# Window attention: queries of strips 2 to 5 written over y between routing and the first pair

## The chip, the cores and the metric

The kernel runs on one core of a Trainium2 chip. A core has five engines with an instruction queue each, worked off in order: PE (TensorE: matmuls and transposes; PEld is its weight loads), DVE (VectorE), ACT (ScalarE), POOL (GpSimd) and SP (SyncE, here used to issue DMAs and to load registers). SBUF is the on-chip memory of 128 partitions, PSUM the small memory that PE writes and DVE and ACT read. Engines wait for each other by semaphores.

The metric is the device time of one execution in microseconds (us), the median of the runs shown. The profile is one execution recorded by the hardware profiler. Its span is the time from the first to the last recorded instruction.

## The reference, cut to what matters

Input and output are 4 images of 64 x 64 pixels with 256 channels. Four residual layers follow one another: two attention layers of the same form, then a Mamba layer and a grouped Mamba layer, which the change does not touch. One attention layer is, with other names shortened:

```python
Z = tanh(w2a @ tanh(w1a @ gn(x)))          # 1x1 convolutions, biases left out
F = sigmoid(w2b @ tanh(w1b @ gn(x)))
y = scan(h = F * h + (1 - F) * Z)          # along H, half of the channels flipped
q, k, v = split(windows(y) @ qkv_w.T)      # 64 windows of 8 x 8 pixels
idx = top_k(mean(q) @ mean(k).T, 4)        # routing: 4 key windows for each window
o = softmax(q @ k[idx].T * SCALE) @ v[idx] # 8 heads of 32 channels, 64 x 256 scores
out = wo_w @ (o + depthwise_conv3x3(v))    # nine taps a channel ("lepe")
x = x + out
```

## The kernel before, in words

The batches run in sequence, and within each the two attention layers and the Mamba layers. All data are float32. 256 channels lie as two halves (`m` = 0, 1) of 128 partitions. The image is cut into 8 **strips** of 8 columns (512 pixels); a strip holds 8 windows. `y`, `x` and `vimg` (the values, with a margin for the 3x3 convolution) stay in SBUF.

The order of instructions on each engine is the order in which the Python code issues them: it is written out by hand, and there is no scheduler. The tile framework adds the semaphore waits; a tile with `bufs=n` has n buffers that are used in turn.

An attention layer has three parts.

**Scan phase** (`scan_phase`, strips s = 0 to 7). Each step makes four pairs of 1x1 convolutions on PE (`conv`, L204: one is 128x512 outputs over 256 inputs), with ACT's tanh as eviction (L283), scans the strip into `y` on DVE, and then makes keys and values of the strip before (`keys_values`), whose rows go to `kv_dram` by DMA (L332, L351). Convolutions use five PSUM buffers with the tag `mm`. From s = 3 on DVE also works on the depthwise convolution of strip s - 3 (`lepe`: 18 steps, 9 for each half; L238 the first tap, L240 the others, accumulated in PSUM). In steps 5 and 6 the queries of strips 0 and 1 are made: `queries` returns an `evict` (two ACT instructions of 64x512, L261) and a `double` (two DMAs of 128 KB, L270). Doubling is there because each of the two 64-partition halves of q has to meet keys that lie in either half of the partitions: `qbuf[s % 2][m]` holds q for both.

**Routing** (`routing`). From window sums of y, q and k means are made, their products, and DVE finds the four best windows (`idx`, L424). After it, DVE makes half m = 0 of strip 5's depthwise convolution (nine taps in PSUM).

**Window phase** (`window_phase`). 32 **pairs** of windows, i = 4 x strip + a. The work of pair i is:

- `indices` (L446): SP loads the eight window numbers into registers. `gather` (L459): eight DMAs of 128 KB fetch keys and values (tile `kv`, six buffers: three pairs). For pairs 0 and 1 ACT's queue issues half of them.
- `scores` (L483): 64 matmuls into two PSUM tiles `sc`, each with one head half h.
- `smallest` (L493): DVE, the minimum of each row of `sc` (q is stored negated), for h = 0 and 1.
- `exps` (L504): eight ACT exponentials with a sum. The last one of each h frees its `sc` tile.
- `normalise`: DVE's reciprocal (L516), then eight POOL products (L519).
- `turn` (L532): 16 PE transposes to PSUM; `turned`: copies to SBUF, two on DVE (L543), two on ACT (L545).
- `values` (L558): 64 matmuls; `own_rows` (L569): DVE adds the result to `vimg`.

In the loop, iteration i issues the gather of pair i + 2, the doubling DMAs, the register loads of i + 3, the scores, minima, exps and normalise of i + 1, and the turn and values of i. Into the same loop go: the queries of strips 2 to 7 (`queries` for m = 0 of strip sj + 2 at a = 3, for m = 1 of strip sj + 1 at a = 0; the evictions at the end of the iteration, the doubling DMAs in the next one, after its gather), the output projection of the strip before (`project`, L204, `add` L579), and the depthwise taps of strips 6 and 7 on POOL (two instructions a tap, L225 and L226). The nine taps of half m = 1 of strip 5 are DVE instructions that add in place in `vimg` (`early`): three between `scores(0)` and the first `smallest`, two at the end of each of the iterations 0, 1 and 2:

```python
mids, ends, left = {}, {0: early[3:5], 1: early[5:7], 2: early[7:]}, []
```

Of the kernel before, what the change touches and what calls it, by code (L numbers as in the profile page):

```python
# [8 lines left out]
F32 = mybir.dt.float32  # L9
BF16 = mybir.dt.bfloat16  # L10
U32 = mybir.dt.uint32
AF = mybir.ActivationFunctionType
# [32 lines left out]
class Net:  # L45
# [33 lines left out]
    def attention_layers(self, x, w_drams, v_drams):  # L79
        tc, nc = self.tc, self.nc  # L80
        with ExitStack() as ctx:
# [13 lines left out]
            nc.gpsimd.memset(vimg[:, :, S + 9 : S + 10, :], 0.0)  # L95


            qbuf = [
                [big.tile([P, 2, NW, 64], F32, name=f"q{i}{m}") for m in range(2)]
                for i in range(2)  # L100
            ]
            layers = []
            for i in range(2):
                vec = wp.tile([P, ATT_VEC], F32, name=f"att_v{i}")
# [93 lines left out]
                return gn(dict(xn={}), s, psum, eng, self.gvar[:, 4 * s : 4 * s + 4])  # L198


            def conv(psum, w, w0, src, m):
                ps = psum.tile([P, NT], F32, tag="mm", name="conv_ps")
                for k in range(2):
                    nc.tensor.matmul(  # L204
                        ps, w[:, k, w0 + m * P : w0 + (m + 1) * P], src[:, k],
                        start=(k == 0), stop=(k == 1),
                    )
                return ps
# [41 lines left out]
            kvd = dram.tile([NW * NW, 64, 2 * C], F32, name="kv_dram")  # L250
            kvd_w = kvd.rearrange("(a b) p f -> b p a f", b=NW)

            def queries(lay, s, m, psum):
                src = y[:, :, strip[s], :].rearrange("p c w h -> p c (w h)")
                ps = conv(psum, lay["wb"], WQ - 4 * C, src, m)
                q = qbuf[s % 2][m]

                def evict():
                    for b in range(2):
                        rows = slice(b * 64, b * 64 + 64)  # L260
                        nc.scalar.activation(  # L261
                            q[rows, b].rearrange("p w (j i) -> p w j i", i=8),
                            ps[rows].rearrange("p (j w i) -> p w j i", j=8, i=8),
                            AF.Identity, bias=lay["neg_bq"][rows, m : m + 1], scale=-SCALE,
                        )

                def double():
                    for b in range(2):
                        here, there = slice(b * 64, b * 64 + 64), slice(64 - b * 64, 128 - b * 64)
                        nc.sync.dma_start(q[there, b], q[here, b])  # L270

                return evict, double


            def scan_phase(lay, work, psum, tail):
# [78 lines left out]
                doubles = []  # L354
                for s in range(NW):
                    g = gn_four(lay, s + 2, lambda: psum) if s + 2 < NW else [lambda: None] * 4
                    taps = lepe(lay, s - 3, psum) if s >= 3 else []
                    g[0]()
                    xn = lay["xn"].pop(s).rearrange("p c w h -> p c (w h)")
                    ha, ha_half = hidden("ha", W1A, xn, AF.Tanh, vec[:, B1A : B1A + 2])  # L360
                    hb, hb_half = hidden("hb", W1B, xn, AF.Tanh, vec[:, B1B : B1B + 2])
                    z, z_half = hidden("z", W2A, ha, AF.Tanh, vec[:, B2A : B2A + 2])

                    f, f_half = hidden("f", W2B, hb, AF.Tanh, lay["half_b2b"], scale=0.5)
                    for half in (ha_half, hb_half):
                        half(0)
# [12 lines left out]
                    g[2]()  # L379
                    f_half(0)  # L380
                    f_half(1)
                    scan(s, f, z)
                    if s:
                        keys_values(s - 1)
                    g[3]()
                    if s >= 5:
                        for _, double in doubles:
                            double()
                    doubles = [queries(lay, s - 5, m, psum) for m in range(2)] if s in (5, 6) else []
                    for evict, _ in doubles:  # L390
                        evict()
                keys_values(NW - 1)


# [34 lines left out]
            def window_phase(lay, work, psum, idx, nxt):  # L429
# [40 lines left out]
                def scores(i):  # L470
                    sj, a = divmod(i, 4)
                    if i < n_pair:
                        for h in range(2):
                            sc[h] = psum.tile([P, 2, 2, 2, P], F32, tag="sc", name="sc", bufs=2)
                        for w in range(2):
                            for m in range(2):
                                for r in range(2):
                                    for h in range(2):
                                        r0 = r * 64 + h * 32
                                        rows = slice(r0, r0 + 32)  # L480
                                        for b in range(2):
                                            k0 = b * P + m * 64
                                            nc.tensor.matmul(  # L483
                                                sc[h][b * 64 : b * 64 + 64, r, w, m, :],
                                                qbuf[sj % 2][m][rows, b, 2 * a + w],
                                                kv[i, w][rows, :, k0 : k0 + 64],
                                                start=True, stop=True,
                                            )
# [111 lines left out]
                mids, ends, left = {}, {0: early[3:5], 1: early[5:7], 2: early[7:]}, []  # L600

                def plan(steps, *where):
                    for f, (at, i) in zip(steps, where):
# [11 lines left out]
                else:  # L615

                    for s in range(NW - 1):
                        i = 4 * s + (10 if s < 5 else 7)
                        plan(stats(s, lambda: psum), (ends, 4 * s + 6), (ends, i), (mids, i + 1),
                             (ends, i + 2), (mids, i + 3), (ends, i + 3), (mids, i + 4))  # L620
                double = None
                for i in range(n_pair):
                    sj, a = divmod(i, 4)
                    add = evict = None
                    gather(i + 2)
                    if double:
                        double()
                        double = None
                    indices(i + 3)
                    scores(i + 1)  # L630
                    smallest(i + 1, 0)
# [50 lines left out]
            for i, lay in enumerate(layers):  # L682
                with tc.tile_pool(name=f"at_a{i}", bufs=1, reuse_waits="tile") as work, tc.tile_pool(
# [1399 lines left out]
```

## Time and profile before

| what | value |
|---|---|
| median of 3 runs | 12012.73 us (11994.23 to 12017.54) |
| the profiled execution | 11996.08 us |
| its span | 11993.8 us |
| TensorE clock granted, mean | 0.93 |
| busy: PE | 9862.3 us (82%) |
| busy: DVE | 9842.8 us (82%) |
| busy: POOL | 8892.2 us (74%) |
| busy: ACT | 7047.9 us (59%) |
| from the first minimum (L493) of a layer to its last, mean of 8 layers | 247.7 us |

The eight attention layers take up about a third of the span; the rest are the Mamba layers, which dominate the page's list of costly groups. A group's line reads: source line, engine, operation, tiles written and read, shapes, count | busy time, mean ns of one | idle time of the engine just before, and what ended most of it. A timeline's line reads: start, duration, engine, line, operation, tiles, shapes, count [idle before <- what ended it]; neighbouring instructions of one kind are drawn together. A line of waits reads: engine and line <- what it waited for: us in total, times, longest. PE's records show two matmuls for each float32 matmul of the program.

### The profile page before, as it was taken

To read this page: it belongs to the slowest core of one execution; us is meant where nothing else is said; L and a number is where in the kernel's file an instruction comes from. 1 tells how busy PE (TensorE), PEld (TensorE's weight loads), DVE (VectorE), ACT (ScalarE), POOL (GpSimd) and SP (SyncE) were. 2 spreads that over 40 slices of the span, in tenths; PEclk is the share of its full clock that TensorE was granted. 3 is DMA by queue.
4 is the path that set the end of the run, shared out by engine and by line. 5 is a ranking of instruction groups with operands and counts; after the bars stand their busy time and mean duration, and the time that the engine had idled before them with its cause. 6 is when DMAs were issued, how large, how long until landed. Compare 5 with 4: busy or idle time off the path is not lost. (4 is left out here: it accounts for less than half of the span.)

```text
span 11993.8 us, 192457 instructions
## 1 busy us (share of the span) xinstructions
PE 9862.3 (82%) x70632; PEld 5605.7 (47%) x71104; DVE 9842.8 (82%) x8322; ACT 7047.9 (59%) x13064; POOL 8892.2 (74%) x6082
## 2 busy tenths in 40 slices
PE   8988887777898788777789878877778987887777
PEld 4554554444455455444445545544444554554444
DVE  6677998998666799899866679989986667998998
ACT  4555555776455555477645655547764565555776
POOL 3666886898466688689846668868974666886897
PEclk9998998999999999899999989989999998998999
DMA  3343444554334355445433444445543343554454
GB/s 92 104 124 134 175 173 146 173 180 161 87 104 126 135 173 175 147 168 179 160 87 104 128 135 173 176 145 169 182 160 84 101 127 134 173 174 147 169 174 155
DMA packets 682830, 1742.11 MB, mean 145 GB/s; under 512 B 89216, under 2 KB 195216, under 8 KB 681632
## 3 DMA queue, kind: packets, MB, share of 16 engines
q1 hardware_dynamic: 676768, 1721.39, 43.4%
q8 instruction: 563, 9.22, 0.3%
q10 hardware_dynamic: 5120, 8.39, 0.3%
q14 instruction: 379, 3.10, 0.1%
HBM read 1601.51 MB, written 94.37 MB: 141 GB/s over the span
## 5 line engine op out<-in xcount | busy, mean ns | idle before, releaser
L927 POOL TENSOR_TENSOR hc<-h,cb 128x1024 f32<-128x1024 f32 x2056 | 4812.2, 2352 | 805.6 <-DVE h L921 358.3
L921 DVE TENSOR_TENSOR_SCAN h<-da,m_state,pb 128x1024 f32<-128x1024 f32 x1248 | 2920.3, 2340 | 163.2 <-DVE pb L915 1.5
L873 PE MATMUL y<-ident,hc 128*128 128x128 f32 x16384 | 2353.3, 291 | 449.9 <-POOL hc L927 351.9
L873 PEld LDWEIGHTS y<-ident,hc 128*128 128x128 f32 x16384 | 2052.7, 151 | 1128.6 <-POOL hc L927 574.4
L915 DVE TENSOR_TENSOR pb<-du,pb 128x1024 f32<-128x1024 f32 x1672 | 2024.8, 1211 | 122.3 <-PE pb L845 98.9
L857 ACT ACTIVATE da<-delta,m_v 128x1024 f32<-128x1024 f32 x1672 | 1898.9, 1141 | 135.8 <-DVE h L921 119.7
L845 PE MATMUL pb<-m_parts,pick 128*128 128x512 bf16 x2840 | 973.1, 413 | 824.0 <-DVE h L921 766.5
L519 POOL TENSOR_SCALAR pr<-pr,sm,zero 128x256 f32<-128x256 f32 x2048 | 1131.3, 569 | 412.1 <-DVE sm L516 362.2
L504 ACT ACTIVATE pr<-sc,mn 128x256 f32<-128x256 f32 x2048 | 959.8, 493 | 717.2 <-DVE mn L493 351.1
L845 PEld LDWEIGHTS <-pick 128*128 128x128 bf16 x3312 | 262.9, 101 | 1770.5 <-DVE h L921 972.9
L921 DVE TENSOR_TENSOR_SCAN h<-da,pb 128x1024 f32<-128x1024 f32 x424 | 969.7, 2287 | 54.9 <-DVE pb L915 1.0
L831 POOL TENSOR_TENSOR bb<-du,bb 128x1024 f32<-128x1024 f32 x376 | 889.0, 2364 | 101.5 <-DMA bb<-m_cd 94.1
L493 DVE TENSOR_REDUCE mn<-sc 128x4 f32<-128x1024 f32 x512 | 609.4, 1219 | 352.7 <-PE sc L483 352.6
L921 DVE TENSOR_TENSOR_SCAN h<-dap,m_state,bb 128x1024 f32<-128x1024 f32 x288 | 672.2, 2334 | 69.2 <-ACT dap L857 48.4
L532 PE MATMUL pt_ps<-ident,pr 128*128 128x128 f32 x4096 | 590.6, 286 | 135.1 <-ACT pts L545 100.3
L204 PE MATMUL conv_ps<-att_y,att_wb 128*128 128x512 f32 x1536 | 691.4, 594 | 5.3 <-DVE gn_mean L151 5.3
L532 PEld LDWEIGHTS pt_ps<-ident,pr 128*128 128x128 f32 x4096 | 459.4, 144 | 361.7 <-POOL tap L225 102.8
L857 ACT ACTIVATE dap<-delta,m_v 128x1024 f32<-128x1024 f32 x376 | 419.7, 1116 | 314.1 <-DVE h L921 232.1
L483 PE MATMUL sc<-kv,q 32*64 32x128 f32 x16384 | 401.4, 296 | 155.7 <-DMA kv<-kv_dram 90.8
L558 PE MATMUL ov_ps<-pts,kv 128*32 128x64 f32 x16384 | 427.8, 231 | 122.1 <-DVE pts L543 74.1
L240 DVE SCALAR_TENSOR_TENSOR lp<-vimg,att_v,lp 128x512 f32<-128x512 f32 x616 | 465.5, 756 | 27.9 <-DVE lp L240 0.5
L204 PE MATMUL conv_ps<-att_xn,att_wa 128*128 128x512 f32 x1024 | 462.7, 605 | 14.2 <-POOL att_xn L180 14.2
(289 smaller groups left out, 16960.3 us busy)
## 6 DMA issues: line engine op xcount, KB each, us to landing
cb<-m_cd SPq DMA_DIRECT2D x2048, 512.0 KB, 3.8
kv<-kv_dram SPq DMA_DIRECT2D x1984, 128.0 KB, 2.7
bb<-m_cd SPq DMA_DIRECT2D x376, 512.0 KB, 5.1
kv_dram<-kst SPq DMA_DIRECT2D x128, 256.0 KB, 3.4
kv_dram<-vn SPq DMA_DIRECT2D x128, 256.0 KB, 4.2
q<-q SPq DMA_DIRECT2D x256, 128.0 KB, 3.0
m_pe<-in_pe_dram SPq DMA_DIRECT2D x32, 512.0 KB, 6.2
out_dram<-yo SPq DMA_DIRECT2D x64, 256.0 KB, 2.4
```

The lines of the kernel that those rows point to most:

```text
L204: nc.tensor.matmul(ps, w[:, k, w0 + m * P : w0 + (m + 1) * P], src[:, k], start=(k == 0), stop=(k == 1),)
L493: nc.vector.tensor_reduce(mn[h], sc[h].rearrange("p r w m n -> p (w m) r n"), AX.XY, ALU.min)
L504: nc.scalar.activation(t[:, g].rearrange("p j r t -> p r j t"), sc[h][:, :, g // 2, g % 2, :].rearrange("p r (j t) -> p r j t", j=2), AF.E ...
L519: nc.gpsimd.tensor_scalar(t[:, g], t[:, g], s[:, g : g + 1], self.zero, ALU.mult, ALU.add)
L532: nc.tensor.transpose(pt[h][j][:, g, :], t[:, g, j].rearrange("p r t -> p (r t)"), self.ident,)
L831: nc.gpsimd.tensor_tensor(pb[i], slots[i][0]["du"], pb[i], ALU.mult)
L845: nc.tensor.matmul(pb[i][:, ss], self.pick[:, n : n + 1].to_broadcast([P, P]), blk["parts"][:, ss], start=True, stop=True,)
L857: nc.scalar.activation(da[i], blk["delta"], AF.Exp, scale=blk["a"](n))
L873: nc.tensor.matmul(blk["y"][:, ss], t[:, ss], self.ident, is_transpose=True, start=(n == 0 and ss.start % NT == 0), stop=(n == DS - 1 and ...
L915: nc.vector.tensor_tensor(pb[i], blk["du"], pb[i], ALU.mult)
L921: nc.vector.tensor_tensor_scan(h[i][:, ss], da[i][:, ss], pb[i][:, ss], state, ALU.mult, ALU.add)
L927: nc.gpsimd.tensor_tensor(hc[i][:, ss], h[i][:, ss], cb[i][:, ss], ALU.mult)
```

## The change

1. The queries of strips 0 to 5, both halves, and of half m = 1 of strips 6 and 7 are written over the strip's own place in `y` (`own`), after all that reads it there; half m = 0 of strips 6 and 7 goes to two small tiles `late_q`. `scores` read them there directly where the half of the partitions is the right one, and from `swap[s % 2]`, which holds only the exchanged halves, where it is not.
2. An eviction is one instruction of 128x512 instead of two of 64x512. `query` takes the engine and the PSUM tag.
3. `double(s)` issues two DMAs of 256 KB for strips 0 to 5 and four of 128 KB for strips 6 and 7. In the scan phase strip 0 is doubled in step 6 and strip 1 in step 7, as before, but with the new tiles.
4. The queries of strips 2, 3 and 4 are made between routing and the window phase: two convolutions, three depthwise taps, two evictions on DVE, three times. Those of strip 5 are made behind `scores(0)`, in two PSUM buffers of the tag `pt`, and evicted by DVE ahead of the reciprocals of pair 0.
5. Only the queries of strips 6 and 7 stay in the pair loop. Doubling of strips 2 to 5 is issued at a = 0 of the strip before, of strips 6 and 7 at a = 1.
6. The nine taps of half m = 1 of strip 5 move from DVE to POOL (17 instructions), ahead of the window phase.

```diff
-            qbuf = [
-                [big.tile([P, 2, NW, 64], F32, name=f"q{i}{m}") for m in range(2)]
-                for i in range(2)
-            ]
+            swap = [big.tile([P, 2, NW, 64], F32, name=f"q_swap{i}") for i in range(2)]
+            late_q = [big.tile([P, NW, 64], F32, name=f"q_late{i}") for i in range(2)]
...
-            def conv(psum, w, w0, src, m):
-                ps = psum.tile([P, NT], F32, tag="mm", name="conv_ps")
+            def conv(psum, w, w0, src, m, tag="mm", **kw):
+                ps = psum.tile([P, NT], F32, tag=tag, name="conv_ps", **kw)
...
-            def queries(lay, s, m, psum):
+            def own(s, m):
+                if m == 0 and s >= NW - 2:
+                    return late_q[s % 2]
+                flat = y[:, m, strip[s], :].rearrange("p r c -> p (r c)")
+                return flat.rearrange("p (w t) -> p w t", t=64)
+
+            def query(lay, s, m, psum, eng=nc.scalar, **kw):
                 src = y[:, :, strip[s], :].rearrange("p c w h -> p c (w h)")
-                ps = conv(psum, lay["wb"], WQ - 4 * C, src, m)
-                q = qbuf[s % 2][m]
+                ps = conv(psum, lay["wb"], WQ - 4 * C, src, m, **kw)
 
                 def evict():
-                    for b in range(2):
-                        rows = slice(b * 64, b * 64 + 64)
-                        nc.scalar.activation(
-                            q[rows, b].rearrange("p w (j i) -> p w j i", i=8),
-                            ps[rows].rearrange("p (j w i) -> p w j i", j=8, i=8),
-                            AF.Identity, bias=lay["neg_bq"][rows, m : m + 1], scale=-SCALE,
-                        )
-
-                def double():
-                    for b in range(2):
-                        here, there = slice(b * 64, b * 64 + 64), slice(64 - b * 64, 128 - b * 64)
-                        nc.sync.dma_start(q[there, b], q[here, b])
-
-                return evict, double
+                    q = own(s, m).rearrange("p w (j i) -> p w j i", i=8)
+                    pq = ps.rearrange("p (j w i) -> p w j i", j=8, i=8)
+                    bias = lay["neg_bq"][:, m : m + 1]
+                    if eng is nc.scalar:
+                        eng.activation(q, pq, AF.Identity, bias=bias, scale=-SCALE)
+                    else:
+                        eng.tensor_scalar(q, pq, -SCALE, bias, ALU.mult, ALU.add)
+
+                return evict
+
+            def double(s):
+                for b in range(2):
+                    here, there = slice(b * 64, b * 64 + 64), slice(64 - b * 64, 128 - b * 64)
+                    if s < NW - 2:
+                        nc.sync.dma_start(
+                            swap[s % 2][there].rearrange("p m w t -> p m (w t)"),
+                            y[here, :, strip[s], :].rearrange("p m r c -> p m (r c)"),
+                        )
+                        continue
+                    for m in range(2):
+                        nc.sync.dma_start(swap[s % 2][there, m], own(s, m)[here])
...
-                    if s >= 5:
-                        for _, double in doubles:
-                            double()
-                    doubles = [queries(lay, s - 5, m, psum) for m in range(2)] if s in (5, 6) else []
-                    for evict, _ in doubles:
-                        evict()
+                    if s >= 6:
+                        double(s - 6)
+                    if s in (5, 6):
+                        for evict in [query(lay, s - 5, m, psum) for m in range(2)]:
+                            evict()
...
-                                                qbuf[sj % 2][m][rows, b, 2 * a + w],
+                                                (own(sj, m) if r == b else swap[sj % 2][:, m])[
+                                                    rows, 2 * a + w
+                                                ],
...
-                early = lepe(lay, NW - 3)[9:]
-                for t in early[:3]:
-                    t()
-                for step in (smallest, exps, normalise):
+                evicts = [query(lay, 5, m, psum, nc.vector, tag="pt", bufs=2) for m in range(2)]
+                for step in (smallest, exps):
                     for h in range(2):
                         step(0, h)
+                for h in range(2):
+                    evicts[h]()
+                    normalise(0, h)
...
-                    if double:
-                        double()
-                        double = None
+                    if a == 0 and 1 < sj + 1 < NW - 2:
+                        double(sj + 1)
+                    elif a == 1 and sj + 1 in (NW - 2, NW - 1):
+                        double(sj + 1)
...
-                    if a == 3 and sj + 2 < NW:
-                        evict, double = queries(lay, sj + 2, 0, psum)
-                    elif a == 0 and 1 < sj + 1 < NW:
-                        evict, double = queries(lay, sj + 1, 1, psum)
+                    if a == 3 and sj + 2 in (NW - 2, NW - 1):
+                        evict = query(lay, sj + 2, 0, psum)
+                    elif a == 0 and sj + 1 in (NW - 2, NW - 1):
+                        evict = query(lay, sj + 1, 1, psum)
...
-                    for t in lepe(lay, NW - 3, psum)[:9]:
+                    taps = lepe(lay, NW - 3, psum)[:9]
+                    for s in range(2, 5):
+                        evicts = [query(lay, s, m, psum, nc.vector) for m in range(2)]
+                        for t in taps[3 * s - 6 : 3 * s - 3]:
+                            t()
+                        for evict in evicts:
+                            evict()
+                    for t in lepe(lay, NW - 3, pool=True)[9:]:
                         t()
```

The tile framework now sees the queries, the convolutions and the doubling DMAs as readers and writers of one tile, `y`: the program that it builds makes ACT's eviction of strip 1's queries in step 6 wait for both DMAs of `double(0)`.

More of the change, by code (lines that the diff above doesn't have):

```diff
@@ L353, in scan_phase @@
                 nc.gpsimd.memset(vimg[:, :, 8:9, :], 0.0)
-                doubles = []
                 for s in range(NW):
@@ L591, in window_phase @@
                 scores(0)
-                early = lepe(lay, NW - 3)[9:]
-                for t in early[:3]:
-                    t()
-                for step in (smallest, exps, normalise):
+                evicts = [query(lay, 5, m, psum, nc.vector, tag="pt", bufs=2) for m in range(2)]
+                for step in (smallest, exps):
                     for h in range(2):
                         step(0, h)
+                for h in range(2):
+                    evicts[h]()
+                    normalise(0, h)
                 taps = [t for s in (NW - 2, NW - 1) for t in lepe(lay, s, pool=True)]
-                mids, ends, left = {}, {0: early[3:5], 1: early[5:7], 2: early[7:]}, []
+                mids, ends, left = {}, {}, []
                 def plan(steps, *where):
@@ L625, in window_phase @@
                     gather(i + 2)
-                    if double:
-                        double()
-                        double = None
+                    if a == 0 and 1 < sj + 1 < NW - 2:
+                        double(sj + 1)
+                    elif a == 1 and sj + 1 in (NW - 2, NW - 1):
+                        double(sj + 1)
                     indices(i + 3)
```

## The prediction

> **What bounds the kernel now.** I read, in this order: the page's groups (which engine does what in a pair), the timeline of a settled pair, the waits of SP's queue, the same timeline at the start of a window phase, fixed windows of the TensorE clock there, and the timeline of scan step s=6. The diff touches only the eight attention layers (4 batches x 2).
>
> Page, costliest groups:
>
> ```profile
> L519 POOL TENSOR_SCALAR pr<-pr,sm,zero 128x256 f32<-128x256 f32 x2048 | 1131.3, 569 | 412.1 <-DVE sm L516 362.2
> L504 ACT ACTIVATE pr<-sc,mn 128x256 f32<-128x256 f32 x2048 | 959.8, 493 | 717.2 <-DVE mn L493 351.1
> L493 DVE TENSOR_REDUCE mn<-sc 128x4 f32<-128x1024 f32 x512 | 609.4, 1219 | 352.7 <-PE sc L483 352.6
> ```
>
> ACT and DVE wait for one another: exps for the minimum, minimum for the scores, scores for the buffers that the last exps free. A settled pair (timeline):
>
> ```profile
> 335.72 1.41 ACT L261 ACTIVATE q<-conv_ps,neg_bq 64x512 f32<-64x512 f32 x2
> 335.94 1.27 PE L483 MATMUL sc<-kv,q 32*64 32x128 f32 x64
> 337.24 2.35 DVE L493 TENSOR_REDUCE mn<-sc 128x4 f32<-128x1024 f32 x2 [1.07 <-PE sc L483]
> 338.07 1.88 PE L204 MATMUL conv_ps<-att_y,att_wb 128*128 128x512 f32 x4
> 338.56 0.47 ACT L504 ACTIVATE pr<-sc,mn 128x256 f32<-128x256 f32 x1 [1.43 <-POOL pr L519]
> ```
>
> Next scores come 6.1 us after the minimum and take 1.3: a floor of 7.38 us a pair. ACT's q eviction lies in the wait for the next minimum (free 1.43 us before the exps at 338.56), the q convolution in PE's wait for normalised rows: both hidden. From the first minimum to the last a layer takes 247.7 us on average, 18.9 above 31 x 7.38. By the starts of the minima, iterations 0 to 3 take 7.80, 8.21, 8.31, 8.20; later ones 4k and 4k+1 about 7.6, 4k+2 and 4k+3 about 8.1. SP's waits:
>
> ```profile
> SPq L459 <- PE ov_ps L558: 242.9, 138, 8.2
> ...
> SPq L270 <- ACT pr L504: 49.1, 108, 1.3
> ```
>
> By its rows in the timeline SP needs about 6.65 us an iteration for 8 gathers and the index loads, and 1.7 more (two q copies and their waits) after which it is over 7.38: the copies at 4k and 4k+1 make the gathers of 4k+3 and 4k+4 late.
>
> Start of layer 1's window phase (timeline), then PE clock by windows (columns: window, length, busy of PE, PEld, DVE, ACT, POOL, PEclk, DMA share, GB/s):
>
> ```profile
> 687.16 0.21 DVE L424 FIND_INDEX8 idx<-top,logit 64x8 uint32<-64x64 f32 x1
> ...
> 694.32 0.54 DVE L238 TENSOR_SCALAR vimg<-vimg,att_v 128x512 f32<-128x512 f32 x1
> 694.90 1.54 DVE L240 SCALAR_TENSOR_TENSOR vimg<-vimg,att_v 128x512 f32<-128x512 f32 x2
> ...
> 697.76 1.98 PE L483 MATMUL sc<-kv,q 32*64 32x128 f32 x56 [0.28 <-DMA kv<-kv_dram]
> 699.77 2.36 DVE L493 TENSOR_REDUCE mn<-sc 128x4 f32<-128x1024 f32 x2 [3.33 <-PE sc L483]
> ```
> ```profile
> 684.27:687.68 3.41, 2.15 (x18) 1.78 (x17) 1.19 (x6) 1.62 (x5) 0.00 (x0) 1.00 0.64 146
> 687.68:691.09 3.41, 0.00 (x0) 0.00 (x0) 3.27 (x5) 0.00 (x0) 0.00 (x0) 0.50 0.70 204
> ...
> 704.74:708.16 3.42, 3.26 (x66) 2.93 (x67) 1.32 (x2) 0.11 (x2) 2.94 (x6) 0.50 0.16 53
> 708.16:711.57 3.41, 1.75 (x20) 1.21 (x18) 2.57 (x5) 3.29 (x14) 0.56 (x2) 1.00 0.00 0
> ```
>
> PE idles from 686.5 to 696.8, so its clock is half for 20.5 us; the first scores take 2.0 instead of 1.26.
>
> Scan step s=6 of layer 0 (timeline): ACT's tanh of ha has 2.5 us in hand before PE's z convolution needs it.
>
> ```profile
> 188.28 3.32 SPq L270 DMA_DIRECT2D q<-q  x4
> 191.72 0.69 ACT L283 ACTIVATE ha<-conv_ps,att_v 128x512 f32<-128x512 f32 x1 [0.97 <-PE conv_ps L204]
> 194.95 3.60 PE L204 MATMUL conv_ps<-ha,att_wa 128*128 128x512 f32 x8
> ```
>
> **The Trainium skill.** "TensorE: Matmul & The Clock Gate", Part 1 (the HAM clock gate): half rate after an idle window of about 3.4 us, full after a busy one. The trace agrees: changes fall on a 3.41 us grid. Recovery came after 3.26 us busy of 3.41, not after 2.92; 1.51 lost the full clock (layer 0), 1.75 kept it. "SBUF — State Buffer", "SBUF: two separate sides": a DVE instruction with two SBUF inputs and a GpSimd instruction that reads SBUF exclude one another. It agrees: a normalise takes 560 ns alone and 905 to 983 beside an in-place tap of DVE. The clock page's section on the array's architecture says that ACT's and DVE's queues are strictly first in, first out; nothing in the trace contradicts it, and part 1 below rests on it: what stands behind a waiting ACT instruction waits, too.
>
> **The change part by part**, per layer, eight times in all.
>
> *1. Scan step 6: a new wait.* Strip 1's q now overwrites y, and its ACT eviction waits for both copies of strip 0's q, which read y. Behind it on ACT stand ha's two tanh, hb's and z's; PE waits for ha. The copies go out at 188.28 as now (2 x 256 KB for 4 x 128). The four land at 191.9 to 193.3; a 256 KB copy lands 3.4 (kst) to 4.2 us (vn) after issue. I take 193.2. Two evictions and two tanh, 4 x 0.70, give ha at 196.0 against 194.95: +1.1. PE runs back to back in the scan, so all of it counts. Ends: 0 (landing at 192.1) to +2.5. Evicting 128 partitions at once saves 4 x 0.68 us of ACT in s=5 and s=6, which waits for PE anyway: nothing.
>
> *2. Routing to first minimum.* DVE loses three in-place taps (0.54 + 1.54 = 2.1 us) and gains six evictions of 128x512 from PSUM (no such row; the 128x512 PSUM copy L543 takes 0.68, L238 0.80; I take 0.70): 4.2. Nine taps take 7.1 us. Order 3 taps, 2 evictions, three times; the first scores' third matmul waits for the fifth eviction: 687.4 + 7.1 + 3.5 = 698.0. PE makes six convolutions at 1.72 us (a pair of them 3.4) from 686.5: done at 696.9 at full clock, ahead of DVE. The window 684.27 to 687.68 is then busy throughout, so I expect full clock; were the next window still half, its 3.41 us of work restore it and PE ends at 698.6. Scores then 1.26 instead of 2.0: minimum at 699.3 against 699.77. I take -0.5; ends -0.8 (DVE's evictions at 0.65) and +0.8 (0.80 and cold). Gathers go out as before, when idx is read.
>
> *3. Strip 5's q* (two convolutions, 3.4 us) follows the first scores on PE, until about 702.7; the second scores' first buffer comes free 3.3 us after the minimum, 702.6. Its two DVE evictions precede the reciprocals in the wait for the exps (DVE idles 0.93 and 1.65 us there). Nothing; cold, the convolutions end about 3.4 us later and still mostly precede the second buffer (5.1 us after the minimum).
>
> *4. Iterations 0 to 3.* All nine in-place DVE taps leave (three above, two each in ends 0, 1, 2, 1.69 us a pair): they delay the minima of iterations 1 to 3 by 0.35 to 0.5 and stretch four normalises from 2.17 to 2.95. With the clock full, the second scores take 1.3 instead of 2.1 and the half-clock window 718.4 to 721.8 need not come. The four took 32.5; at 7.0 + 3 x 7.4 they would be 29.2. I take -2.6; ends -3.3 and -0.9 (taps alone, clock as now).
>
> *5. Nine taps on POOL.* 17 instructions, 0.77 or 1.18 us, about 17.9 us, from POOL's last copy at 681.3 to 699.2. The first normalise comes at 703.3 (now) or 702.8: 3.6 us of cover; what exceeds it costs the first pair in full. Beside them DVE's taps accumulate in PSUM, with one SBUF input: they measure 755 ns beside POOL and 756 without. Nothing; upper end +0.5.
>
> *6. Pairs.* Removed 20 evictions of ACT and eight convolutions: hidden, nothing. On SP, strips 2 to 5 now have two copies of 256 KB at 4k and none at 4k+1; issue of one is 0.55 (q) to 1.0 us (vn), about the 1.4 of two small ones now. So of two late iterations (0.55 each) one goes: 4 x -0.55 = -2.2. Strips 6 and 7 put four copies at 4k+1: 2.8 us at once into a slack of 0.5 plus the idle of a pair, one iteration +1.7 for two of 0.6: +0.5 each. Sum -1.2; ends -3.5 (the two copies fit the slack) and +0.8.
>
> Sum: 1.1 - 0.5 - 2.6 - 1.2 = -3.2 a layer, x8 = -26. The profiled execution took 11996.1 (span 11993.8), so 11970 for it; the median 12012.7 lies 16.6 above, so **11987**. A change under 0.2% (24 us, 3 us a layer) can't be told from none.
>
> **Rivals.**
> *A, same: clock and SP give little.* For it: layer 0's half-clock time began only 3.4 us after the idling, so the grid's phase counts, and the second scores leave PE idle for 1.7 us. Against: eight convolutions in 16 us. Entry +0.1, early iterations -0.9, SP -0.5, scan +1.1: -0.2, 12011.
> *B, slower: the ACT stall of step 6.* Each us that the copies land after 193.2 costs 8. The parts of 2, 4 and 6 together give -4.3, so from a landing at 196.4 the change loses. For it: the copies stand behind two 256 KB stores with 4.2 us of landing, and PE has only five PSUM buffers for convolutions. Against: now all four landed by 193.3 with the same bytes. At 199.5: +7.4 - 4.3 = +3.1, 12038.
> *C, faster: SP relieved.* If the pair of large copies fits SP's slack, both late iterations of strips 2 to 5 go, -4.4, less 1.0 for 6 and 7: part 6 is -3.4, the sum -5.4, 11969. For it: one copy more or less is all the difference between 6.65 and 8.35. Against: 4k+2 is late after the first pair of copies alone.
> *D: POOL's taps run late.* Ending 5 us later they pass the cover by 1.4: -1.8, 11998. POOL is idle there now, so little speaks for it.
>
> **How the numbers follow.** Forecast 0.47 (its own range 11973 to 12002), A 0.25, B 0.08, C 0.16, D 0.04. The forecast's case lies a little over half beyond -24, so faster is 0.27 of it, all of C and 0.03 from A's better fringe, 0.46; slower 0.09, nearly all of B; same the rest. Range: C's better end (sum -7.5: 11953, less a few) to A with a stall of 2.5 (sum +1.2: 12022): 11950 to 12025.
>
> **What would show it.** Step 1: idle before the ACT eviction of strip 1 put down to the copies, and a PE gap of about 1 us before z in s=6 of all layers. Step 2: first minimum 11.9 us after idx instead of 12.4, PEclk 1.0 from routing on. Step 4: iterations 0 to 3 near 7.4. Step 6: 4k+3 of strips 2 to 5 near 7.5, iterations 22, 23, 26, 27 with one long. Wrong if the clock drops in spite of the convolutions, if the scan step loses over 2 us, or if normalise waits for POOL's taps.

## The result

The changed kernel takes **12040.18 us** (median of 10 runs, 12024.69 to 12056.11) against 12011.51 us before (10 runs): ratio 1.0024, 95% interval 1.0016 to 1.0032. The forecast was 11987 with a range of 11950 to 12025. The change made the kernel slower by 29 us where 26 us of gain were expected.

The profiled execution took 12037.48 us, its span is 12035.7. The trace can be cut by stage (means over the eight attention layers, us; "scan" from the z convolution of step 0 to the found indices, "entry" from there to the first minimum, "loop" from the first minimum to the last; the rest of the execution, mostly Mamba layers, varies by some 10 us between executions of the same code and was 8445 before, 8444 after):

| stage | before | after | difference | forecast |
|---|---|---|---|---|
| scan | 183.43 | 184.81 | +1.4 | +1.1 |
| entry | 12.46 | 11.82 | -0.6 | -0.5 |
| loop | 247.68 | 252.31 | +4.6 | -3.8 |
| sum x 8 | | | +43 | -26 |

So two of the three came out as worked out, and the pair loop went the other way by 8.4 us a layer. (The single profiled executions are 42 us apart, the medians 29; a second measurement of the same kernel, below, gave 38. The profiled execution of before, 11996 us, is among the fastest of its ten, so the column of before may be up to 2 us a layer too low, an estimate from 12012 - 11996 over eight layers.)

**The page, costliest groups**, the three lines that answer to those shown of before:

```profile
L514 ACT ACTIVATE pr<-sc,mn 128x256 f32<-128x256 f32 x2048 | 956.3, 490 | 849.3 <-DVE mn L503 453.2
L529 POOL TENSOR_SCALAR pr<-pr,sm,zero 128x256 f32<-128x256 f32 x2048 | 1105.7, 556 | 328.6 <-DVE sm L526 316.2
L503 DVE TENSOR_REDUCE mn<-sc 128x4 f32<-128x1024 f32 x512 | 609.3, 1219 | 402.2 <-PE sc L491 400.5
```

The instructions themselves are as short as before, POOL's products even shorter (556 for 569 ns: no DVE tap beside them). What grew is waiting: exps for the minimum 351 to 453 us, minima for PE's scores 353 to 400 us. PE's scores are what comes late.

**Start of the window phase, layer 1** (timeline, then windows of PE's clock with the columns as before: window, length, busy of PE, PEld, DVE, ACT, POOL, clock, DMA share, GB/s):

```profile
691.57 10.57 PE L202 MATMUL conv_ps<-att_y,att_wb 128*128 128x512 f32 x24
...
692.26 0.21 DVE L432 FIND_INDEX8 idx<-top,logit 64x8 uint32<-64x64 f32 x1
...
701.78 1.41 DVE L268 TENSOR_SCALAR att_y<-conv_ps,neg_bq 128x512 f32<-128x512 f32 x2
...
704.42 3.70 PE L202 MATMUL conv_ps<-att_y,att_wb 128*128 128x512 f32 x8
704.49 2.35 DVE L503 TENSOR_REDUCE mn<-sc 128x4 f32<-128x1024 f32 x2 [1.30 <-PE sc L491]
```
```profile
692.21:695.63 3.42, 3.42 (x10) 1.51 (x9) 3.35 (x7) 0.00 (x0) 3.13 (x4) 1.00 0.71 208
...
712.69:716.11 3.42, 1.68 (x24) 1.22 (x28) 1.94 (x4) 3.42 (x14) 1.20 (x3) 1.00 0.00 0
716.11:719.52 3.41, 3.41 (x116) 3.01 (x116) 0.18 (x1) 0.80 (x4) 3.19 (x7) 0.50 0.30 76
719.52:722.93 3.41, 1.36 (x18) 1.08 (x11) 3.17 (x4) 1.85 (x8) 0.68 (x1) 1.00 0.63 184
```

The six convolutions keep the full clock through the entry, and the first minimum comes 12.0 us after the indices in this layer, as worked out. But at 716 the clock is at half again: it was lost after a window with 1.68 us of work in 3.41.

**A pair of strip 2 in the loop** (timeline, PE and DVE, of after, pair 8; then of before, pair 9; both pairs had a query convolution in before):

```profile
768.69 2.36 DVE L503 TENSOR_REDUCE mn<-sc 128x4 f32<-128x1024 f32 x2
...
771.66 1.06 PE L542 MATMUL pt_ps<-ident,pr 128*128 128x128 f32 x8 [1.97 <-ACT pts L555]
```
```profile
769.73 2.36 DVE L493 TENSOR_REDUCE mn<-sc 128x4 f32<-128x1024 f32 x2 [1.05 <-PE sc L483]
770.57 1.88 PE L204 MATMUL conv_ps<-att_y,att_wb 128*128 128x512 f32 x4
...
772.70 1.06 PE L532 MATMUL pt_ps<-ident,pr 128*128 128x128 f32 x8 [0.25 <-ACT pts L545]
```

Where before had a query convolution, PE now waits 1.97 us for ACT's copy. That stretch was there before (1.88 us of convolution and 0.25 us idle); the convolution only filled it. The windows of after around it:

```profile
770.72:774.13 3.41, 1.87 (x36) 1.41 (x40) 2.01 (x5) 3.41 (x15) 3.33 (x6) 1.00 0.64 182
774.13:777.55 3.42, 3.42 (x117) 2.92 (x105) 0.30 (x2) 0.61 (x4) 3.38 (x7) 0.50 0.19 47
777.55:780.96 3.41, 1.49 (x13) 1.28 (x13) 3.16 (x4) 2.21 (x9) 0.55 (x1) 1.00 0.67 197
780.96:784.37 3.41, 3.35 (x77) 2.46 (x83) 0.97 (x3) 2.52 (x11) 2.60 (x5) 0.50 0.74 226
```

With 1.87 us of work in a window, the next runs at half; that one is busy throughout (3.42 us), because the matmuls take longer at half rate, and the clock comes back; then the next thin window loses it again. In before the window that holds the convolution has 3.16 us of work, and the clock stays:

```profile
769.59:773.00 3.41, 3.16 (x22) 1.83 (x16) 3.27 (x4) 2.01 (x9) 2.19 (x4) 1.00 0.50 148
```

Counted over 85 such windows from 20 us ahead of the first minimum in each of the eight layers, the clock fell (from full to half) 38 times before and 93 times after.

**SP's waits and scan step 6** (waits; timeline of layer 0):

```profile
SPq L467 <- PE ov_ps L568: 301.8, 181, 7.1
...
SPq L282 <- ACT pr L514: 6.8, 15, 1.7
```
```profile
187.18 2.12 SPq L276 DMA_DIRECT2D q_swap<-att_y  x2
...
192.51 1.26 ACT L266 ACTIVATE att_y<-conv_ps,neg_bq 128x512 f32<-128x512 f32 x2 [8.12 <-DMA q_swap<-att_y]
193.25 1.98 PE L202 MATMUL conv_ps<-att_xn,att_wa 128*128 128x512 f32 x4 [0.96 <-ACT att_y L266]
...
195.07 3.60 PE L202 MATMUL conv_ps<-ha,att_wa 128*128 128x512 f32 x8
```

SP waits longer for free buffers (302 for 243 us), and its copies wait less for ACT (6.8 for 49.1 us), so it has more time in hand than before; a slower PE also frees the buffers later, so these lines alone do not show that the copies cost SP less. In the scan, ACT stands 8.12 us before strip 1's evictions until the copies have landed, and PE waits for it.

### The profile page after: what moved, and what is told of

Same layout as the page of the kernel before. It is cut to its first block, busy times and chain, and to the rows that moved or that the text cites. A ratio compares the mean times of both kernels' runs of the same rounds, so it can differ in the third digit from the quotient of the medians.

```text
span 12035.7 us, 192733 instructions
## 1 busy us (share of the span) xinstructions
PE 9941.4 (83%) x71104; PEld 5654.5 (47%) x71104; DVE 9831.1 (82%) x8314; ACT 6920.6 (58%) x12872; POOL 8991.5 (75%) x6218
## 5 line engine op out<-in xcount | busy, mean ns | idle before, releaser
L863 PE MATMUL pb<-m_parts,pick 128*128 128x512 bf16 x3312 | 1079.8, 410 | 841.6 <-DVE h L939 777.6
L529 POOL TENSOR_SCALAR pr<-pr,sm,zero 128x256 f32<-128x256 f32 x2048 | 1105.7, 556 | 328.6 <-DVE sm L526 316.2
L875 ACT ACTIVATE dap<-delta,m_v 128x1024 f32<-128x1024 f32 x376 | 419.8, 1116 | 311.1 <-DVE h L939 242.3
L568 PE MATMUL ov_ps<-pts,kv 128*32 128x64 f32 x16384 | 466.6, 248 | 111.2 <-DVE pts L553 64.5
```

The lines of the kernel that those rows point to most:

```text
L529: nc.gpsimd.tensor_scalar(t[:, g], t[:, g], s[:, g : g + 1], self.zero, ALU.mult, ALU.add)
L863: nc.tensor.matmul(pb[i][:, ss], self.pick[:, n : n + 1].to_broadcast([P, P]), blk["parts"][:, ss], start=True, stop=True,)
L875: nc.scalar.activation(da[i], blk["delta"], AF.Exp, scale=blk["a"](n))
```

## The experiments

The theory formed from this: **the convolutions that the change took out of the pair loop had kept PE's clock at full**; without them it falls in the iterations 4, 5, 8, 9, 12, 13, 16 and 17, where they had stood. The rival: **the copies of 256 KB hold up the gathers on SP**. Iterations that are slow for the one reason hide the other, so both had to be switched on their own. All ratios are to the kernel before, measured beside it on the same chip. "Loop" is the stage of the table above (us a layer, one profiled execution each).

| kernel | median us | ratio, 95% interval | loop | falls of the clock |
|---|---|---|---|---|
| after | 12040.2 | 1.0024 (1.0016 to 1.0032) | 252.3 | 93 |
| after, again | 12042.9 | 1.0030 (1.0018 to 1.0041) | 252.7 | 95 |
| b_noconv | 12030.8 | 1.0023 (1.0015 to 1.0032) | 253.1 | 97 |
| a_warm | 12026.1 | 1.0017 (1.0010 to 1.0024) | 251.6 | 46 |
| a_order | 12029.6 | 1.0020 (1.0014 to 1.0027) | 250.7 | 93 |
| a_both | 12014.3 | 1.0005 (0.9997 to 1.0014) | 251.2 | 47 |
| a_spread | 11970.4 | 0.9967 (0.9955 to 0.9979) | 244.5 | 39 |
| a_spread_cold | 12013.7 | 1.0010 (1.0001 to 1.0018) | 250.0 | 87 |
| a_nocopy | 11942.7 | 0.9948 (0.9934 to 0.9961) | 242.3 | 42 |
| a_warm2 | 11980.2 | 0.9981 (0.9971 to 0.9990) | 246.8 | 16 |
| a_full | 11945.4 | 0.9950 (0.9937 to 0.9964) | 240.8 | 10 |
| a_full_dve | 11956.2 | 0.9963 (0.9950 to 0.9977) | 242.6 | 10 |
| b_warm | 11990.3 | 0.9987 (0.9979 to 0.9995) | 246.4 | 17 |

Mean length of the iterations 4 to 27 by their place in the strip (us). Here, as in the prediction, iteration k runs from the first minimum of pair k to that of pair k + 1, so a convolution that the code issues in its iteration i, behind the minima of pair i + 1, lies in iteration i + 1:

| kernel | 4k | 4k+1 | 4k+2 | 4k+3 |
|---|---|---|---|---|
| before | 7.57 | 7.67 | 8.19 | 8.16 |
| after | 8.14 | 8.14 | 7.89 | 8.15 |
| b_noconv | 8.23 | 8.17 | 7.90 | 8.00 |
| a_both | 7.61 | 7.65 | 8.66 | 8.19 |
| a_nocopy | 7.57 | 7.62 | 7.78 | 7.74 |
| a_full | 7.52 | 7.68 | 7.95 | 7.87 |

**b_noconv: the kernel before without the convolutions.** The queries of strips 2 to 5 and their evictions are left out of the loop, for both halves; the copies stay.

```diff
                     if a == 3 and sj + 2 < NW:
-                        evict, double = queries(lay, sj + 2, 0, psum)
+                        if sj + 2 < NW - 2:
+                            double = again(sj + 2, 0)   # the copies alone
+                        else:
+                            evict, double = queries(lay, sj + 2, 0, psum)
...
```

> The kernel before with the eight convolutions and evictions of the queries of strips 2 to 5 left out of the pair loop, the copies of 128 KB kept (these strips then use strip 0's and 1's queries). Clock theory: half-rate loads and long iterations appear around 4k as in the changed kernel, pair loop up by 2 to 5 us a layer, time 12030 to 12050 although the kernel does less. Copy theory: nothing on the path leaves or comes, 12005 to 12012.

It does less and takes 12030.8, 27 us more than before. The classes turn into those of the changed kernel, almost number for number, and the clock falls 97 times. In the eight iterations named above the clock is at half for 28.1 us a layer, 24.7 in the changed kernel and 0.4 in before. Nothing of the change's writing over y, swap tiles, copies of 256 KB or taps on GpSimd is in this kernel: leaving out the convolutions and their evictions is enough to make the loop as slow as the changed one's. That it is the convolutions and not the evictions is shown by the next run, which puts only the convolutions back.

**a_warm: idle convolutions put back into the changed kernel.**

```diff
+            def warm(lay, psum):
+                conv(psum, lay["wb"], 0, lay["wb"][:, :, 0:NT], 0)   # nobody reads the result
...
+                    if (a == 3 and sj + 2 < NW - 2) or (a == 0 and 1 < sj + 1 < NW - 2):
+                        warm(lay, psum)
```

> The changed kernel with one idle convolution on PE (128x512 over 256 inputs, weights by weights, its result never read) put back at each of the eight places of the pair loop from which the queries of strips 2 to 5 were taken (a = 3 and a = 0). Clock theory (the queries' convolutions kept PE busy enough for the full clock; without them iterations 4k and 4k+1 fall to half rate): iterations 3, 4, 5, 8, 9, 12, 13, 16, 17 lose their 6.3 us a layer over the kernel before, pair loop from 252.3 to about 246.5 us, time about 11995. Copy theory (the 256 KB copies at 4k hold up the gathers): no change, 12040, and the half-rate loads may go without the time.

Neither. The half-rate time in those eight iterations went (24.7 us a layer to none), and with it the length of 4k and 4k+1 (8.14 each to 7.63 and 7.65); but 4k+2 went from 7.89 to 8.73 and the loop lost 0.7 us, not 6. The waits of PE, the kernel before first, then the changed kernel, then a_warm, tell what took over:

```profile
PE pt_ps L532 <- ACT pts L545: 100.3, 166, 2.4
```
```profile
PE pt_ps L542 <- ACT pts L555: 199.4, 181, 2.0
...
PE sc L491 <- DMA kv<-kv_dram: 21.4, 31, 1.6
```
```profile
PE pt_ps L545 <- ACT pts L558: 105.3, 170, 2.0
...
PE sc L494 <- DMA kv<-kv_dram: 50.3, 64, 2.5
```

PE's idle time before the transposes goes back to what it was before, and its wait for gathered keys more than doubles: with a fast PE the gathers are what comes last. So both theories seemed to hold, each hiding the other; the next runs test that.

**a_order: strip 1's evictions ahead of strip 0's copies in scan step 6**, and **a_both**: this with the idle convolutions.

```diff
-                    if s >= 6:
-                        double(s - 6)
                     if s in (5, 6):
                         for evict in [query(lay, s - 5, m, psum) for m in range(2)]:
                             evict()
+                    if s >= 6:
+                        double(s - 6)
```

> The changed kernel with the two evictions of strip 1's queries issued ahead of the copies of strip 0's queries in scan step 6. Theory of the ACT stall: step 6 to step 7 falls from 26.3 back to 24.9 us a layer, time lower by 8 x 1.4 = 11 us, 12029; pair loop unchanged at 252.3. If the stall is hidden after all or only moves: within 4 us of 12040.

> Both edits: the idle convolutions and the evictions ahead of the copies. Clock theory and stall add up: scan as before, pair loop about 246.5, entry 11.8, so about 11984, faster than the kernel before. Copy theory: 12029.

The step from z of 6 to z of 7 takes 26.31 us in after and 24.91 in a_order, in every layer, the value of before; a_both, measured together with a_warm, is 12 us below it. The stall was worth about what its trace said, 8 x 1.4 = 11 us. a_both missed its 11984 by what a_warm had missed.

**a_nocopy, a_spread: the copies**, on the base of a_both. The first leaves the copies of strips 2 to 7 out of the loop, the second issues one half of them at a = 0 and the other at a = 1:

```diff
-                    if a == 0 and 1 < sj + 1 < NW - 2:
-                        double(sj + 1)
-                    elif a == 1 and sj + 1 in (NW - 2, NW - 1):
-                        double(sj + 1)
+                    if a < 2 and 1 < sj + 1 < NW - 2:
+                        double(sj + 1, bs=[a])     # one DMA of 256 KB
+                    elif a < 2 and sj + 1 in (NW - 2, NW - 1):
+                        double(sj + 1, ms=[a])     # two of 128 KB
```

> The changed kernel with idle convolutions and early evictions (12014), with the copies of the swapped halves of strips 2 to 7 left out of the pair loop (these strips then use strip 0's and 1's). Copy theory (what is left of the loss is SP: a pair of 256 KB copies with the slower register loads behind it, or four copies in a row, holds up the gathers): iterations 4k+2 and 4k+3 fall from 8.66 and 8.19 to about 7.6, pair loop from 251.2 to about 241 us, time about 11935. If those iterations are long for another reason: 12000 to 12014.

> The same base (12014) with the copies spread: one of 256 KB at a = 0 and one at a = 1 for strips 2 to 5, two of 128 KB at a = 0 and two at a = 1 for strips 6 and 7. Copy theory: the burst on SP falls from about 2.0 us to 1.0 for strips 2 to 5, and for 6 and 7 to what the kernel before has; pair loop down by 3 to 4 us a layer, time about 11986. If SP's total and not the burst counts: no change, 12010 to 12018.

Both came: 11942.7, and 11970.4 with all copies still made, more than the expected gain (11986). Without copies 4k+2 falls from 8.66 to 7.78. SP's own timeline shows the burst; a_both first, then before:

```profile
3276.68 1.39 SPq L279 DMA_DIRECT2D q_swap<-att_y  x2
3280.11 11.93 SPq L470 DMA_DIRECT2D kv<-kv_dram  x16
```
```profile
3277.61 1.18 SPq L270 DMA_DIRECT2D q<-q  x2
3280.05 3.23 SPq L459 DMA_DIRECT2D kv<-kv_dram  x5
```

The two large copies are issued in 1.39 us, hardly more than two small ones (1.18). But between their end and the next gather, where SP loads the next two windows' numbers, 2.04 us pass, against 1.26. The first register load behind a pair of 256 KB copies took 945 ns on average in a_both and the second 508; behind a pair of 128 KB copies in before it was 490 and 335, behind a gather 304 each. It is not the size of one copy: behind a single copy of 256 KB in a_spread the loads took 304 and 322 ns. The next gather is issued late by the difference, and the last gather of pairs 7, 11, 15 and 19 goes out 5.2 to 5.7 us behind the first minimum of the pair before in a_both, 4.0 to 4.1 in a_spread. The gathers do not travel longer (the median from issue to landing is 2.7 us in before and a_both, 2.8 in a_spread and a_nocopy), which speaks against transfers that hold each other up. In a_spread PE waits little for either (its waits):

```profile
PE pt_ps L545 <- ACT pts L558: 93.5, 168, 2.0
...
PE sc L494 <- DMA kv<-kv_dram: 16.6, 33, 1.4
```

The wait for keys is 16.6 us where a_warm has 50.3.

**a_spread_cold: the copies spread, the clock left to fall.** After and a_order gave the corners without either; this is the missing one.

> The changed kernel with the early evictions and the spread copies, but without any idle convolution. With the clock kept full, spreading was worth 44 us (12014 to 11970). If half-rate PE and late gathers add up: the same 44 us off 12030, about 11985. If they are two limits of which the later counts (a pair slowed by PE gives SP the time to catch up): most of the gain stays hidden and only iterations 22, 23, 26 and 27, which are not half-rate, get shorter, 1 to 2 us a layer, 12013 to 12022.

> The changed kernel itself, unchanged, as the base for the other run of this call and for the single edits. From the traces it should be 11 us above the version with the early evictions (12030), and its ratio to the kernel before 1.0024 as measured first.

The medians make a square, all with the early evictions: neither 12029.6, full clock alone 12014.3, spread alone 12013.7, both 11970.4. Alone each is worth 15 or 16 us, together 59 (by the ratios, which take out the chips' own differences, 0.15, 0.10 and 0.53%). The profiled loops, one execution each, are starker: against a_order the full clock alone changes a layer by +0.4 us, spreading alone by -0.7, both by -6.3. A pair that PE slows gives SP the time in which the gathers catch up: the iterations 6, 7, 10, 11, 14, 15, 18 and 19, behind the slow ones, take 62.4 us together in a_order and 66.8 in a_both. Only with both removed does the loop become shorter. The forecast of 12013 to 12022 for two limits of which the later counts was met, that of their adding up (11985) was not; but the place that it named was wrong: iterations 22, 23, 26 and 27 take 33.7 us together, 33.3 in a_order. after_again confirms the base: 12042.9, 13 us above a_order where the traces say 11.

**a_warm2, a_full: the clock elsewhere.** a_warm2 (on a_both, where the code's iteration 3 has one already) also puts an idle convolution into the code's iterations 0, 1, 2, 27 and 28, 13 a layer in all; a_full has this and the spread copies.

```diff
+                    if i < n_pair - 1 and (
+                        sj == 0 or (a == 3 and sj + 2 not in (NW - 2, NW - 1))
+                        or (a == 0 and sj + 1 not in (NW - 2, NW - 1))
+                    ):
+                        warm(lay, psum)
```

> The same base (12014) with further idle convolutions in iterations 0 to 3, 27 and 28, where half-rate weight loads are left. Clock theory: iterations 1 to 3 fall from 8.1 to 8.6 to about 7.7, 28 and 29 from 9.0 and 9.2 to about 8.1: 3 to 4 us a layer, time about 11985. If SP sets these iterations too, the half-rate loads go and the time stays: 12005 to 12014.

> Both of the last two on the same base. Both theories: 6 to 7 us a layer off 12014, about 11960, and so faster than the kernel before. If only one holds: about 11985.

11980.2 and 11945.4, close to what was expected (11985 and 11960). Iterations 0 to 3 take 29.95 us together in a_warm2, for 32.3 in after. a_full is faster than the kernel before by 0.50% (0.36 to 0.63), 63 us by the medians. Its clock falls 10 times in the counted windows, four of them behind the last minimum; within the loop it is at half for 2.6 us a layer, 45.7 in after. The loop takes 240.8 us.

**a_full_dve: GpSimd's nine taps back on DVE**, in a_full.

> The version with all edits (11945) with the nine taps of strip 5 moved back from GpSimd to DVE, as in the kernel before: three between the first scores and the first minimum, two at the end of each of the iterations 0, 1, 2. If the prediction's part 4 was right about the taps themselves: first minimum about 1.5 us later (DVE's sixth eviction ends near 698.5 and three taps take 2.1), iterations 1 to 3 longer by 0.3 to 0.5 each, 2.7 us a layer, time about 11967. If they lie beside other work: within 6 us of 11945.

11956.2: 11 us by the medians and 16 by the ratios, less than the 22 expected, and outside the 6 us of the other case. The two intervals overlap (0.9937 to 0.9964 and 0.9950 to 0.9977), so the times alone hardly tell the two apart. By the trace the first minimum is 0.75 us later and iterations 0 to 3 take 1.4 us more. So moving the taps was worth having, by an amount that is known only roughly.

**b_warm: the kernel before with five idle convolutions**, in iterations 0, 1, 2, 27 and 28.

> The kernel before with one idle convolution in each of the iterations 0, 1, 2, 27 and 28, nothing else changed. Clock theory: the half-rate weight loads of iterations 1 to 3, 28 and 29 go; 1 to 3 shorten by about 0.4 each (DVE's in-place taps still delay them), 28 and 29 by 1.4 together, so 2 to 3 us a layer, time 11985 to 11995 although the kernel does more. If SP sets these iterations: 12005 to 12012.

11990.3, ratio 0.9987 (0.9979 to 0.9995): the kernel that does more is faster. The kernel before had the same loss, only less of it.

## Why the prediction was wrong, step by step

*1. The scan's new wait: right.* +1.1 forecast, +1.40 measured, and gone with the order of two statements. The path was a little different: PE did not first wait for ha but for one of its five PSUM buffers, which the stalled eviction held (0.96 us, the line above). The evictions began 5.3 us after the first copy's issue, where the forecast had 4.9.

*2. and 3. Entry: right.* Full clock, DVE's evictions 0.745 us for the 0.70 taken, first minimum 0.6 us earlier for 0.5. Strip 5's convolutions cost nothing; iteration 0 took 7.06 us for the 7.0 expected.

*4. Iterations 0 to 3: failed.* Forecast 32.5 to 29.9, measured 32.3. The step assumed that a clock that is full at the entry stays so: "the half-clock window 718.4 to 721.8 need not come". It came (716.11 to 719.52 above). The prediction had named the sign itself: "if the clock drops in spite of the convolutions". The size was right for the condition: with the clock nearly always full in these iterations they took 29.95. The taps' own share, at the entry and here together, is 1.4 to 2.2 us a layer by a_full and a_full_dve.

*5. GpSimd's taps: right.* In layer 1 they ended at 704.0, and POOL's first product at 708.2 waits for DVE's reciprocal, with 4.2 us idle before it.

*6. The pairs: failed*, in the sentence "Removed 20 evictions of ACT and eight convolutions: hidden, nothing". They were hidden, and they were not nothing: their work was PE's activity. The prediction had the rule and the numbers for it (1.51 us lost the clock, 1.75 kept it) and used them for the entry alone; it never asked what a window of the loop would hold when a convolution of 1.88 us is gone. By a window of before that holds one, 3.16 - 1.88 leaves 1.3, under both numbers. (The two are no threshold: the window shown above lost the clock with 1.87.) b_noconv puts a price on it: 27 us. Summed by groups of iterations, the loop's difference to before is (us a layer, one execution each, with the caution on before given under the result):

| iterations | term of the forecast | forecast | after | a_both | a_spread |
|---|---|---|---|---|---|
| 0 to 3 | taps gone, full clock (step 4) | -2.6 | -0.2 | -0.4 | -0.7 |
| 4, 5, 8, 9, 12, 13, 16, 17 | convolutions gone | 0 | +5.8 | -0.4 | -0.7 |
| 6, 7, 10, 11, 14, 15, 18, 19 | one late iteration for two | -2.2 | -2.6 | +1.9 | -2.3 |
| 20 to 27 | copies of strips 6 and 7 | +1.0 | +1.3 | +1.7 | +0.1 |
| 28 to 30 | none | 0 | +0.4 | +0.7 | +0.3 |
| sum | | -3.8 | +4.6 | +3.5 | -3.2 |

The convolutions priced at nothing cost 5.8 us; the gain of step 4 that did not come is the next in size.

The rest of step 6, the copies, was wrong in a second way that the clock covered up. Two 256 KB copies were costed by their issue, 1.4 us; with the slower register loads behind them they hold SP for longer, all at once, and with a full clock 4k+2 takes 8.66 us instead of the 8.19 of before. That their forecast of -2.2 agrees with the changed kernel's -2.6 is luck: there the half-rate iterations ahead gave SP time, and at full clock the same copies cost 1.9. Where they are spread the relief that was forecast is there: a_spread, which has the change's copies, has -2.3 in these iterations and a loop 3.2 us under the kernel before's. The +1.0 for strips 6 and 7 was about right.

*The rivals.* A (the clock gives little) had the right engine, but the wrong sign for the loop: it was drawn as a gain that fails to come, and half-rate pairs beyond iteration 3 were in no case. B's mechanism was real, but the copies held ACT about 0.4 us longer than figured, not the 3 us from which the change would have lost; slower came from another place. C (both large copies fit SP's slack) is refuted by a_both, where 4k+2 grows. D did not come: 4.2 us of cover were left.

## What to carry to other kernels

Before moving matmuls out of a loop because they are hidden there, sum PE's busy time in the clock's windows (3.41 us here) with and without them: if a window falls to about half (1.9 us here), the loop's other matmuls run at half rate, and the hidden work was paying for them. Where two limits lie close together, taking away either shows little; take both away before judging a change worthless. And price DMAs in a queue by when the next one of that queue goes out, not by their issue alone: here two copies of 256 KB together held it up, and in two different iterations they did not.

## What the runs showed of the hardware

- The clock needs no idle window to fall. After a window at full clock it fell with 1.07 to 2.08 us of PE work in 3.41 (93 cases in the changed kernel) and stayed with 1.53 to 3.42 (472 cases, 95% of them over 2.19). Over all fourteen traces, 1.9 us of work sorts all but 100 of the 8438 windows at full clock, but single ones fell with up to 2.61 and stayed with 1.5: around half to six tenths, and not by busy time alone. "TensorE: Matmul & The Clock Gate" of the Trainium skill, in Part 1 (the HAM clock gate), names an idle window as what loses the clock; here the measurement decides.
- In the changed kernel the clock came back only after a window with at least 2.95 us of work (93 cases; 2.91 over all traces, and windows with up to 3.35 stayed at half). At half rate these loops mostly reach that at once: so it alternates, window by window.
- Work whose result nobody reads can shorten a kernel: five convolutions a layer, 1.88 us each at full clock, took 16 us off the kernel before (b_warm).
- A register load on SP right behind two copies of 256 KB in a row took 945 ns (a_both), behind two of 128 KB 490 (before), behind four of 128 KB 301 (a_both), behind one of 256 KB 304 (a_spread), behind a gather 304. Why is open.
